# A transformer decoder layer: softmax sums inverted once a token tile and spread by way of DRAM, cross-attention in halves and quarters of the array, spline rows by indirect DMA

## The chip, the cores and the metric

The kernel runs on one NeuronCore of one Trainium2 chip. The metric is the device time of one execution in microseconds (us); less is better. The engines are PE (TensorE, matrix products), DVE (VectorE), ACT (ScalarE), POOL (GpSimd) and SP (SyncE, which here only issues DMAs). PE writes to PSUM; POOL doesn't read PSUM in this kernel.

## The reference, cut to what matters

All data is float32: four sequences of 1024 tokens with 256 features. Three sublayers follow each other, each on a normalized copy of `x` and each added to `x`:

```python
# 1. self-attention: 16 query heads, 4 key/value heads, head size 64
scores = einsum('bhqd,bhkd->bhqk', xq, xk)
probs  = softmax(scores)
out    = einsum('bhqk,bhkd->bqhd', probs, xv).reshape(B, S, 1024) @ o_w.T + o_b
# 2. cross-attention: 16 heads of size 16, 64 context tokens, masked
attn = softmax(where(mask, -inf, (q @ k.T) * 0.25))
out  = (attn @ v).reshape(b, sq, 256) @ Wout + bout
# 3. routed spline layer: each token picks one of 64 tiles
tile_idx = cluster_idx * 8 + local_idx            # two stages of argmax over calibrated scores
hh  = relu(einsum('ni,nig->ng', comp, spline_w1[tile_idx]) + spline_b1[tile_idx])
mag = einsum('ng,ngo->no', hh, spline_w2[tile_idx]) + spline_b2[tile_idx]
y   = xf + mag * directions[tile_idx] * output_scale
y   = (y - mean(y)) / sqrt(var(y) + eps) * gamma + beta
```

## The kernel before, in words

**Order of the work.** Nothing is emitted directly. Every piece of work is given to `Flow.add` (line 93) as a task with an engine, an estimated cost, a key (its place in the run), the tiles that it reads and writes, and the buffers that it holds. `Flow.order` (line 120) then plays all tasks through with those costs and emits, on each engine, whatever can start first; a `lag` is the delay that it assumes until another engine sees the result. So a changed cost or dependence reorders every engine's instructions. On the chip each engine works through its own list in order.

**Self-attention.** A sequence `b` has 8 token tiles `qt` of 128 tokens. A tile's 16 heads lie in 8 pairs of 64 partitions (`QC`), and two pairs make a `duo` (line 551): 4 duos for a tile, 32 for a sequence, 128 in all. For each pair there is one score task (line 577): four matmuls, two for each half of the array, each 64 rows by 512 columns, into two PSUM tiles `s` of 128x1024. There are two such tiles, so the next score task needs both back. DVE takes the negated row maximum `nmax` (line 591), and ACT the exponential with its row sum (line 597), which goes into `sums` and the probabilities into `prob`. In three of four duos DVE turns 32x32 blocks (line 606) and SP carries them with 16 DMAs into `probT` (line 633); in the fourth (`by_array`) PE transposes (`ptp`, line 616) and ACT copies (line 620). Then `av` (line 656) multiplies by the values, with the two heads of a pair in the two column halves of the array.

**Sums.** For each duo, DVE inverts its four sums (`rsum`, line 676). PE spreads them over partitions: four matmuls of a repeated column with the identity (`rb`, line 682). DVE copies that out of PSUM (line 691) and multiplies `av` by it into `heads` (line 695). After four duos `project` (line 702) multiplies by `wo` (`po`, line 709), adds the bias on DVE (712) and `x` on POOL (715).

**Cross-attention** (line 780) runs for two token tiles at a time. `context` builds a block-diagonal `kblk` with 8 heads per 128 partitions (`XC`), so the scores `xs` (line 819) are two matmuls of 128 rows and 512 columns for each tile. DVE adds the mask (822) and takes the maximum (834), POOL subtracts it (837), ACT takes the exponential (841), PE transposes (`pxt`, 854) and ACT copies to `xpT` (857). `xav` (line 870) then takes `xpT` as weights and `vblk` as moving operand: eight matmuls with 34 columns, 2 x 16 values and, per head, the sum. DVE inverts and divides (873, 874), PE transposes the result (`pxo`, 888), ACT copies (891) and `pxp` (900) projects.

**Spline layer** (`feed_forward`, line 991). Four token tiles at a time, at the end two. After the products with `cw1` (`pch`), `cw2` (`pcomp`) and the signatures (`pr`, line 1045) a chain of small DVE operations calibrates and picks a tile; `hot` (1075) is its one-hot row. PE transposes it (`pht`, 1089), ACT copies (1092), and a matmul with the table picks each token's row (`pg`, 1097), which ACT copies to `par` (1100).

**Normalizing** (`layernorm`, line 390): statistics on DVE (401, 402), the inverse root on POOL (406, 407), and `(x - mean) * rs` on DVE (412).

The lines of the softmax sums that the change replaces:

```python
add("DVE", 0.17, at, inverse, [ss.part(4 * e + k) for k in range(4)], [rs])
add("PE", 0.6, at + 1, spread, [rs], [pr], holds=[rb])
add("DVE", 0.42, at + 1, evict_rb, [pr], [rb])
add("DVE", 0.42, at + 1, evict, [av, rb], [heads[b, qt].part(e)])
```

Of the kernel before, what the change touches and what calls it, by code (L numbers as in the profile page):

```python
# [10 lines left out]
F32 = mybir.dt.float32  # L11
# [6 lines left out]
P = 128  # L18
# [174 lines left out]
def decoder(  # L193
# [28 lines left out]
    ps_o = ctx.enter_context(tc.tile_pool(name="ps_o", bufs=1, space=PSUM))  # L222

# [4 lines left out]
            heads=1, rb=1, rsum=2, res=1, ln=2, xxT=1, xqT=1, kblk=1, vblk=1, xkt=1, xvt=1, xsc=1,  # L228
            xmx=2, xpT=1, xrs=2, xo=1, xoT=1, xf=1, fxT=1, hT=1, sc=1, comp=2, cal=1, fm=4, hot=1, hotT=1,
            par=1, hh=1, mag=2,  # L230
        ),
        {"p1", "ln", "res", "rb", "rsum", "nmax"},
# [48 lines left out]
    tab, tab_ = load("tab", [NTILES, GT], table, "SP", -30, 8)  # L281
# [18 lines left out]
    for i in range(NCL):  # L300
        nc.gpsimd.memset(falling[:, i : i + 1], float(NCL - i))

    own = const.tile([P, XC], F32, name="own")
    nc.gpsimd.memset(own, 1.0)
    nc.gpsimd.affine_select(
        out=own, in_=own, compare_op=ALU.is_ge, fill=0.0, base=0, pattern=[[-XD, XC]], channel_multiplier=1
    )
    nc.gpsimd.affine_select(
        out=own, in_=own, compare_op=ALU.is_ge, fill=0.0, base=XD - 1, pattern=[[XD, XC]], channel_multiplier=-1
    )  # L310
# [5 lines left out]
    add("DVE", 0.2, 2, lambda: nc.vector.tensor_scalar(keep, kmask8, -1.0, 1.0, ALU.mult, ALU.add), [kmask_], [keep_])  # L316
# [40 lines left out]
    quants = buf("xo", work, 2, DC, NTILES, name="quants")  # L357
# [32 lines left out]
    def layernorm(key, name, src, dst, w, reads, writes):  # L390
# [13 lines left out]
        def rsqrt():  # L404
            _, mv, rs = st.t
            nc.gpsimd.tensor_scalar(rs, mv[:, :, 1], EPS, None, ALU.add)
            nc.gpsimd.tensor_tensor(rs, rs, minus_half.to_broadcast([P, w]), ALU.pow)

        def apply():
            _, mv, rs = st.t  # L410
            for t in range(w):
                nc.vector.tensor_scalar(dst(t), src(t), mv[:, t, 0:1], rs[:, t : t + 1], ALU.subtract, ALU.mult)
# [3 lines left out]
        add("DVE", 0.41 * w, key, apply, [st, *reads], writes)  # L416
# [134 lines left out]
    def duo(b, d):  # L551
# [3 lines left out]
        if e == 0:  # L555
            sums[b, qt] = buf("sums", small, H, name=f"sums_{b}_{qt}")
            heads[b, qt] = buf("heads", work, QC, P, name=f"heads_{b}_{qt}")
        ss = sums[b, qt]
        prob = Buf("prob", lambda: work.tile([P, 4 * S], F32, tag="prob", name=f"prob_{b}_{d}"))
# [8 lines left out]
        for i in range(2):  # L568
# [17 lines left out]
            for z in range(2):  # L586
                k = 2 * c + z
# [58 lines left out]
        for part in range(2):  # L646
            def values(part=part):
# [20 lines left out]
                holds=[heads[b, qt]],  # L668
            )

        rs = buf("rsum", small, 4, name=f"rsum_{b}_{d}")
        pr = psum1(f"rb_{b}_{d}")
        rb = buf("rb", work, 2 * P, name=f"rb_{b}_{d}")

        def inverse():
            nc.vector.reciprocal(rs.t, ss.t[:, 4 * e : 4 * e + 4])

        def spread():
            for i in range(2):
                for z, r in enumerate(halves):  # L680
                    k = 2 * i + z
                    mm(  # L682
                        pr.t[r, i * P : (i + 1) * P],
                        lhsT=rs.t[:, k : k + 1].to_broadcast([P, HD]),
                        rhs=ident,
                        start=True,
                        stop=True,
                    )

        def evict_rb():  # L690
            nc.vector.tensor_copy(rb.t, pr.t[:, : 2 * P])

        def evict():
            to = heads[b, qt].t[:, 2 * e : 2 * e + 2, :].rearrange("p c q -> p (c q)")
            nc.vector.tensor_tensor(to, av.t, rb.t, ALU.mult)  # L695

        add("DVE", 0.17, at, inverse, [ss.part(4 * e + k) for k in range(4)], [rs])
        add("PE", 0.6, at + 1, spread, [rs], [pr], holds=[rb])
        add("DVE", 0.42, at + 1, evict_rb, [pr], [rb])
        add("DVE", 0.42, at + 1, evict, [av, rb], [heads[b, qt].part(e)])  # L700

    def project(b, qt):
        at = float(b * NT * QC + qt * QC + QC + 1)
        hT, xb = heads[b, qt], x_part(b, qt)
        po, t = psum1(f"po_{b}_{qt}"), buf("res", work, D, name=f"res_{b}_{qt}")
        for part in range(2):
            def out_rows(part=part):
                for c in range(4 * part, 4 * part + 4):
                    mm(po.t[:, :D], lhsT=hT.t[:, c, :], rhs=wo[:, c, :], start=(c == 0), stop=(c == QC - 1))  # L709

            add("PE", 1.75, at, out_rows, [hT.part(e) for e in range(4)] + [wo_] + [po] * part, [po], holds=[t])
# [9 lines left out]
    def context(b, at):  # L721


        kblk = kblks[b] = buf("kblk", big, DC, XC, SK, name=f"kblk_{b}")
        vblk = vblks[b] = buf("vblk", big, XH // 2, 2, XD + 1, name=f"vblk_{b}")
# [18 lines left out]
        def block_k(c):  # L744
            nc.vector.tensor_tensor(
                kblk.t[:, c],
                kt.t[:, c, :].unsqueeze(1).to_broadcast([P, XC, SK]),
                own.unsqueeze(2).to_broadcast([P, XC, SK]),
                ALU.mult,
            )  # L750
# [13 lines left out]
        def block_v():  # L764
            vt4 = vt.t.rearrange("p (g t d) -> p g t d", t=2, d=XD)
            for half in range(2):
                r = slice(half * SK, (half + 1) * SK)
                nc.vector.tensor_scalar(vblk.t[r, :, half, :XD], vt4[r, :, half, :], keep[r, b : b + 1], None, ALU.mult)
                nc.vector.tensor_copy(vblk.t[r, :, half, XD], keep[r, b : b + 1].to_broadcast([SK, XH // 2]))
# [10 lines left out]
    def cross_attention(b, t0, at):  # L780
# [31 lines left out]
        for k in range(TX):  # L812
            now = at + 2 + 3 * k
            sc = buf("xsc", work, XH, SK, name=f"xsc_{name}_{k}")
            for c in range(DC):
                ps = psum1(f"xs_{name}_{k}_{c}")

                def scores(c=c, ps=ps, k=k):
                    mm(ps.t, lhsT=qT.t[:, c, k * P : (k + 1) * P], rhs=kblk.t[:, c], start=True, stop=True)  # L819

                def masked(c=c, ps=ps, sc=sc):
                    nc.vector.tensor_tensor(  # L822
                        sc.t[:, XC * c : XC * (c + 1), :],
                        ps.t.rearrange("p (h k) -> p h k", k=SK),
                        mneg[:, b, :].unsqueeze(1).to_broadcast([P, XC, SK]),
                        ALU.add,
                    )

                add("PE", 0.9, now, scores, [qT, kblk], [ps], holds=[sc])
                add("DVE", 0.68, now, masked, [ps, mneg_], [sc])  # L830
# [14 lines left out]
            add("ACT", 1.07, now, exponential, [sc], [sc])  # L845
            pT = buf("xpT", work, XH // 2, P, name=f"xpT_{name}_{k}")
            for g in range(2):
# [12 lines left out]
                add("ACT", 0.6, now + 2, evict, [pt], [pT])  # L860
            av = psum1(f"xav_{name}_{k}")
            rs = buf("xrs", small, XH, name=f"xrs_{name}_{k}")
            o = buf("xo", work, D, name=f"xo_{name}_{k}")

            def rows_of(av=av):
                return av.t[:, : XH * (XD + 1)].rearrange("p (h d) -> p h d", h=XH)

            def values(av=av, pT=pT, rows_of=rows_of):
                for g in range(XH // 2):
                    mm(rows_of(av)[:, 2 * g : 2 * g + 2, :], lhsT=pT.t[:, g, :], rhs=vblk.t[:, g], start=True, stop=True)  # L870

            def divide(av=av, rs=rs, o=o, rows_of=rows_of):
                nc.vector.reciprocal(rs.t, rows_of(av)[:, :, XD])
# [402 lines left out]
```

## Time and profile before

| | |
|---|---|
| median of 3 runs | 1993.22 us (1990.15 to 1993.29) |
| profiled execution | 1997.92 us, of which the span is 1996.2 us |
| mean granted TensorE clock | 0.965 |
| busy | PE 93%, DVE 77%, ACT 48%, POOL 13% |
| DMA | 220.92 MB, of which `probT` 1536 transfers of 128 KB |

In a row of costly groups one reads: the line of the kernel, the engine, the operation, the tile written and those read (with the numbers of buffers left out), the shapes, how often, then the busy time of the group and the mean of one in ns, then the idle time of the engine ahead of it and what ended most of that. A float32 matmul stands in the records as two instructions, a transpose by identity as one. A row of the chain in order of time has its start, how long it lasted, and what ran.

### The profile page before, as it was taken

To read this page: it belongs to the slowest core of one execution; us is meant where nothing else is said; L and a number is where in the kernel's file an instruction comes from. 1 tells how busy PE (TensorE), PEld (TensorE's weight loads), DVE (VectorE), ACT (ScalarE), POOL (GpSimd) and SP (SyncE) were. 2 spreads that over 40 slices of the span, in tenths; PEclk is the share of its full clock that TensorE was granted. 3 is DMA by queue.
4 is the path that set the end of the run, shared out by engine and by line. 5 is a ranking of instruction groups with operands and counts; after the bars stand their busy time and mean duration, and the time that the engine had idled before them with its cause. 6 is when DMAs were issued, how large, how long until landed. Compare 5 with 4: busy or idle time off the path is not lost.

```text
span 1996.2 us, 30371 instructions
## 1 busy us (share of the span) xinstructions
PE 1864.4 (93%) x11204; PEld 1114.0 (56%) x11204; DVE 1538.9 (77%) x2447; ACT 964.2 (48%) x1730; POOL 267.2 (13%) x422
## 2 busy tenths in 40 slices
PE   7899999999999999989999999989999999997973
PEld 4455555655566555556556555655556655564542
DVE  4767787897788878787778878887778877778853
ACT  2545455555445555545445545454545554553431
POOL 1000101030010301121000311103001030010322
PEclk9899999999999999989999999998999999998975
DMA  3555554454455455545454456535455435545510
GB/s 132 127 127 137 127 132 109 105 121 108 104 127 117 94 122 123 123 110 127 96 116 107 95 128 137 122 75 127 96 122 127 101 91 127 113 100 127 119 24 5
DMA packets 87859, 220.92 MB, mean 111 GB/s; under 512 B 26336, under 2 KB 36896, under 8 KB 87712
## 3 DMA queue, kind: packets, MB, share of 16 engines
q1 hardware_dynamic: 85440, 212.42, 47.3%
q0 software_dynamic: 1168, 4.19, 0.6%
q8 instruction: 89, 1.46, 0.3%
q10 hardware_dynamic: 1104, 2.37, 0.3%
q14 instruction: 58, 0.48, 0.1%
HBM read 13.37 MB, written 4.19 MB: 9 GB/s over the span
## 4 chain that ended last, share of the span: by engine, by line
PE 81%; DVE 12%; ACT 3%; DMA 1%; issue 1%; SPq 1%; POOL 1%; POOLq 0%; ACTq 0%; DVEq 0%
PE s L577 25%; PE av L656 22%; DVE nmax L591 6%; PE pq L530 5%; PE po L709 5%; PE ptp L616 5%; PE rb L682 2%; PE xav L870 2%; PE xs L819 2%; PE pxq L797 2%; ACT prob L597 2%; PE pv L502 2%; DVE prob L606 1%; PE pk L479 1%; PE pg L1097 1%; PE pxp L900 1%
## 5 line engine op out<-in xcount | busy, mean ns | idle before, releaser
L597 ACT ACTIVATE prob<-s,nmax 128x1024 f32<-128x1024 f32 x512 | 569.2, 1115 | 581.0 <-DVE nmax L591 571.3
L591 DVE TENSOR_REDUCE nmax<-s 128x1 f32<-128x1024 f32 x512 | 602.1, 1217 | 211.4 <-PE s L577 210.6
L577 PE MATMUL s<-kT,qT 64*128 64x512 f32 x2048 | 545.4, 621 | 9.3 <-ACT prob L597 9.0
L656 PE MATMUL av<-probT,vn 128*64 128x256 f32 x4096 | 479.6, 385 | 2.7 <-DMA probT<-prob 2.5
L606 DVE STREAM_TRANSPOSE prob<-prob 128x1024 f32<-128x1024 f32 x384 | 460.3, 1225 | 20.5 <-ACT prob L597 15.3
L656 PEld LDWEIGHTS av<-probT,vn 128*64 128x64 f32 x4096 | 284.0, 137 | 204.1 <-issue 70.5
L577 PEld LDWEIGHTS s<-kT,qT 64*128 64x128 f32 x2048 | 196.2, 187 | 216.6 <-issue 170.2
L620 ACT COPY probT<-ptp 128x512 f32<-128x512 f32 x256 | 138.9, 594 | 127.7 <-PE ptp L616 127.7
L616 PE MATMUL ptp<-ident,prob 128*128 128x128 f32 x1024 | 147.6, 281 | 20.5 <-ACT probT L620 5.0
L616 PEld LDWEIGHTS ptp<-ident,prob 128*128 128x128 f32 x1024 | 109.9, 141 | 76.4 <-issue 31.2
L530 PE MATMUL pq<-ln_T,wq 128*128 128x256 f32 x512 | 132.2, 407 | 4.2 <-DMA wq<-in_w_qT 3.7
L837 POOL TENSOR_TENSOR xsc<-xsc,xmx 128x1024 f32<-128x1024 f32 x32 | 61.0, 1908 | 497.0 <-DVE xmx L834 252.6
L709 PE MATMUL po<-wo,heads 128*128 128x256 f32 x512 | 121.1, 386 | 1.9 <-DVE xsc L822 1.8
L530 PEld LDWEIGHTS pq<-ln_T,wq 128*128 128x128 f32 x512 | 99.2, 202 | 32.8 <-issue 15.0
L709 PEld LDWEIGHTS po<-wo,heads 128*128 128x128 f32 x512 | 94.2, 190 | 34.5 <-issue 15.9
L715 POOL TENSOR_TENSOR x<-x,res 128x256 f32<-128x256 f32 x32 | 23.3, 728 | 620.9 <-DVE res L712 516.6
L597 ACT ACTIVATION_READ_ACCUMULATOR prob<-s,nmax 128x1 f32 x512 | 100.8, 197 | 0.0
L541 ACT ACTIVATE qT<-pq,bqs,qscale 128x256 f32<-128x256 f32 x128 | 65.3, 563 | 49.6 <-PE pq L530 49.2
L695 DVE TENSOR_TENSOR heads<-av,rb 128x256 f32<-128x256 f32 x128 | 53.0, 414 | 46.7 <-PE av L656 45.6
L682 PEld LDWEIGHTS rb<-ident,rsum 128*64 128x64 f32 x1024 | 54.6, 136 | 59.0 <-issue 45.4
L682 PE MATMUL rb<-ident,rsum 128*64 128x128 f32 x1024 | 83.3, 284 | 4.2 <-DVE xres L903 4.2
L819 PE MATMUL xs<-kblk,xq 128*128 128x512 f32 x128 | 67.9, 653 | 1.7 <-ACT xq L806 1.7
(162 smaller groups left out, 1526.9 us busy)
## 6 DMA issues: line engine op xcount, KB each, us to landing
probT<-prob SPq DMA_DIRECT2D x1536, 128.0 KB, 2.3
ln_n<-in_x SPq DMA_DIRECT2D x16, 256.0 KB, 3.1
x<-in_x SPq DMA_DIRECT2D x8, 512.0 KB, 4.2
out<-ln_n POOLq DMA_DIRECT2D x7, 512.0 KB, 3.5
wo<-in_w_oT SPq DMA_DIRECT2D x1, 1024.0 KB, 13.3
wq<-in_w_qT ACTq DMA_DIRECT2D x1, 1024.0 KB, 9.6
rowv<-in_rows ACTq DMA_DIRECT2D x1, 774.0 KB, 11.7
xwkv<-in_xw_kv SPq DMA_DIRECT2D x1, 512.0 KB, 13.1
```

What stands on the lines that cost most here:

```text
L530: mm(pq.t[:, 2 * P * k : 2 * P * (k + 1)], lhsT=wq[:, dc, (c + k) * P : (c + k + 1) * P], rhs=xTs[b].t[:, dc, 2 * P * w : 2 * P * (w + 1)] ...
L541: nc.scalar.activation(qTs[b, w, c + k].t, pq.t[:, 2 * P * k : 2 * P * (k + 1)], AF.Identity, bias=bqs[:, c + k : c + k + 1], scale=qscale,)
L577: mm(ps[z].t[:, 512 * g : 512 * (g + 1)], lhsT=q.t[r, (qt % 2) * P : (qt % 2 + 1) * P], rhs=kT.t[r, 512 * g : 512 * (g + 1)], start=True, ...
L591: nc.vector.tensor_reduce(nmax.t, ps[z].t, AX.X, ALU.max, negate=True)
L597: nc.scalar.activation(weights(prob.t, z, i), src, AF.Exp, bias=nmax.t, accum_out=ss.t[:, k : k + 1])
L606: nc.vector.transpose(t, t)
L616: flip(pt.t[:, j * P : (j + 1) * P], weights(prob.t, z, i)[:, kc * P : (kc + 1) * P], ident)
L620: nc.scalar.copy(to[:, z, 4 * g : 4 * g + 4, i, :], pt.t.rearrange("p (c q) -> p c q", q=P))
L656: mm(av.t[r, :], lhsT=vns[b, kc // 2].t[:, kc % 2, j * HD : (j + 1) * HD], rhs=rhs, start=(kc == 0), stop=(kc == NT - 1),)
L682: mm(pr.t[r, i * P : (i + 1) * P], lhsT=rs.t[:, k : k + 1].to_broadcast([P, HD]), rhs=ident, start=True, stop=True,)
L709: mm(po.t[:, :D], lhsT=hT.t[:, c, :], rhs=wo[:, c, :], start=(c == 0), stop=(c == QC - 1))
L819: mm(ps.t, lhsT=qT.t[:, c, k * P : (k + 1) * P], rhs=kblk.t[:, c], start=True, stop=True)
```

## The change

- **Sums.** `rb` is made once for a token tile instead of for each duo. DVE inverts all 16 sums, PE flips the 128x16 tile, ACT copies it to `rsT`, SP writes it to DRAM (`rsD`), and two more DMAs on SP read it back, each repeated over 64 partitions. `av` is copied by ACT without a factor to a buffer of its duo (five of them); POOL multiplies that by `rb`. Within a tile the sums are put in the order of the array half (`z * QC + c`).
- **Cross-attention.** `kblk` holds four heads for each half of the partitions, so that `xs` is four matmuls of 64 rows and 256 columns, the two halves into two PSUM tiles. The sums of the exponentials are taken by two halvings on POOL, a short reduction and a reciprocal on DVE, and a product on POOL, ahead of the transposes. In `xav` the values become the weights: eight matmuls of 32 columns of the array each, at column 0, 32, 64 or 96, with 128 moving columns. The result is transposed already, so `pxo` goes. `keep` is set up with five operations instead of one.
- **Spline rows.** The index of the tile is computed, and POOL's indirect DMA fetches each token's row from the table in DRAM. The one-hot transpose, its copy, the products with the table and their copies go, and so does the load of the table.
- **Normalizing.** The last step moves to ACT as `rs * x + (-mean * rs)`; POOL computes the added term with two more operations.

```diff
-            nc.vector.tensor_tensor(to, av.t, rb.t, ALU.mult)
-        add("DVE", 0.17, at, inverse, [ss.part(4 * e + k) for k in range(4)], [rs])
-        add("PE", 0.6, at + 1, spread, [rs], [pr], holds=[rb])
-        add("DVE", 0.42, at + 1, evict_rb, [pr], [rb])
-        add("DVE", 0.42, at + 1, evict, [av, rb], [heads[b, qt].part(e)])
+            nc.scalar.copy(hd.t.rearrange("p c q -> p (c q)"), av.t)
+        add("ACT", 0.45, at + 1, evict, [av], [hd])
...
+        def flip_inverse():
+            flip(pr.t[:H, :P], rs.t, ident)
+        def spread(z, r):
+            nc.sync.dma_start(out=rb.t[r], in_=rD.t[z : z + 1].to_broadcast([HD, QC, P]))
+        def divide(e):
+            nc.gpsimd.tensor_tensor(hT[e].t, hT[e].t, rb.t[:, 2 * e : 2 * e + 2, :], ALU.mult)
+        add("DVE", 0.17, at - 4, inverse, [sums[b, qt].part(k) for k in range(H)], [rs])
+        add("PE", 0.2, at - 4, flip_inverse, [rs], [pr], holds=[rT])
+        add("ACT", 0.3, at - 4, lambda: nc.scalar.copy(rT.t, pr.t[:H, :P]), [pr], [rT], holds=[rD, rb])
+        add(
+            "SP", 0.5, at - 4,
+            lambda: nc.sync.dma_start(out=rD.t.rearrange("z c q -> (z c) q"), in_=rT.t), [rT], [rD], lag=2.5,
+        )
+        for z, r in enumerate(halves):
+            add("SP", 0.5, at - 4, lambda z=z, r=r: spread(z, r), [rD], [rb.part(z)], lag=2.5)
+        for e in range(QC // 2):
+            add("POOL", 0.6, at - 1, lambda e=e: divide(e), [rb.part(0), rb.part(1), hT[e]], [hT[e]])
...
-                    mm(ps.t, lhsT=qT.t[:, c, k * P : (k + 1) * P], rhs=kblk.t[:, c], start=True, stop=True)
+                for c in range(DC):
+                    for z, r in enumerate(halves):
+                        mm(
+                            ps[z].t[:, 256 * c : 256 * (c + 1)],
+                            lhsT=qT.t[r, c, k * P : (k + 1) * P],
+                            rhs=kblk.t[r, c],
...
+            add("POOL", 1.6, now + 1, add_up, [sc], [half], holds=[rs])
+            add("DVE", 0.6, now + 1, inverse, [half], [rs])
+            add("POOL", 1.9, now + 1, divide, [sc, rs], [sc])
...
-                    mm(rows_of(av)[:, 2 * g : 2 * g + 2, :], lhsT=pT.t[:, g, :], rhs=vblk.t[:, g], start=True, stop=True)
+                        mm(
+                            av.t[32 * j : 32 * (j + 1), P * c : P * (c + 1)],
+                            lhsT=vblk.t[:, 4 * c + j].rearrange("p t d -> p (t d)"),
+                            rhs=pT.t[:, 4 * c + j, :],
+                            tile_position=(0, 32 * j),
...
-            add("PE", 0.3, now + 4, flip_o, [o], [pt], holds=[oT])
-            add("ACT", 0.38, now + 4, evict_o, [pt], [oT])
+                "ACT", 0.4, now + 3,
+                lambda av=av, oT=oT: nc.scalar.copy(oT.t.rearrange("p c q -> p (c q)"), av.t[:, :D]), [av], [oT],
...
-        add("DVE", 0.41 * w, key, apply, [st, *reads], writes)
+        add("ACT", 0.45 * w, key, apply, [st, *reads], writes)
...
-            add("PE", 0.6, at + 11, gather, [hotT, tab_], [pg], holds=[par])
-            add("ACT", 0.45, at + 11, evict, [pg], [par.part(t)])
+                nc.gpsimd.indirect_dma_start(
+                    out=par.t[:, t, :],
+                    out_offset=None,
+                    in_=table,
+                    in_offset=bass.IndirectOffsetOnAxis(ap=hot.t[3][:, t : t + 1], axis=0),
+                )
+            add("POOL", 1.2, at + 11, gather, [hot], [par.part(t)], lag=3.0)
```

## The prediction

> **What bounds the kernel now.** I read the page's shares first, then the chain that ended last, then that chain in order of time, and last the timeline around one score task.
>
> ```profile
> span 1996.2 us, 30371 instructions
> PE 1864.4 (93%) x11204; PEld 1114.0 (56%) x11204; DVE 1538.9 (77%) x2447; ACT 964.2 (48%) x1730; POOL 267.2 (13%) x422
> PE 81%; DVE 12%; ACT 3%; DMA 1%; issue 1%; SPq 1%; POOL 1%; POOLq 0%; ACTq 0%; DVEq 0%
> L682 PE MATMUL rb<-ident,rsum 128*64 128x128 f32 x1024 | 83.3, 284 | 4.2 <-DVE xres L903 4.2
> L819 PE MATMUL xs<-kblk,xq 128*128 128x512 f32 x128 | 67.9, 653 | 1.7 <-ACT xq L806 1.7
> ```
>
> PE is the bound: 93% busy and 81% of the chain. But its busy time counts pipeline ends twice. What a task really holds PE for is read from the chain in order of time, here from 780 us on (start, us, what):
>
> ```profile
> 780.03 1.90 PE xav L870 x16
> ...
> 783.81 1.92 PE s L577 x8
> ...
> 787.61 1.91 PE xs L819 x4
> 789.52 0.22 PE pxo L888 x2
> ...
> 795.31 0.59 PE rb L682 x8
> ```
>
> Priced so, every PE task of the program comes to 1783 us, so PE has 213 us with nothing to do: before the first score task (38.6 us), after the last (from 1895.7 us), and in between. What makes the holes in between is the ring score, maximum, exponential, next score (two PSUM buffers `s`):
>
> ```profile
> 730.11 1.99 PE L577 MATMUL s<-kT,qT 64*128 64x512 f32 x8
> 732.12 2.35 DVE L591 TENSOR_REDUCE nmax<-s 128x1 f32<-128x1024 f32 x2 [1.48 <-PE s L577]
> 733.44 1.11 ACT L597 ACTIVATE prob<-s,nmax 128x1024 f32<-128x1024 f32 x1 [4.70 <-DVE nmax L591]
> 734.55 1.10 ACT L597 ACTIVATE prob<-s,nmax 128x1024 f32<-128x1024 f32 x1
> ```
>
> PE leaves the score at 732.02 and its buffers are free at 735.7: 3.7 us, which PE must fill with other work. I took the PE timeline apart at the 256 score tasks and set the other work ("filler") of each of the 255 gaps beside the gap's length less 1.92. With 2.5 to 3.3 us of filler (33 gaps) a gap lasted 0.8 us beyond it; at 3.3 to 4.2 us (31 gaps) 0.5; at 4.2 to 5.6 (131 gaps) 0.4; above that nothing. In the 14 gaps above 7 us it lasted 2.9 longer, 40 us in all: PE stands there in order behind the routing of the feed-forward.
>
> ```profile
> PE pht L1089 <- DVE hot L1075: 30.1, 5, 12.8
> ```
>
> All excess comes to 138 us. So between scores: 255 x 1.92 + 1230 filler + 138 = 1857 us, which is 1895.7 - 38.6.
>
> **The change, part by part.** PE work. `rb` goes: 128 tasks of 0.59 or 0.44 (where its neighbour has its array shape), -72. In its place 32 flips of a 128x16 tile, at most 0.25 each by the 0.147 of one 128x128 flip (0.59 for four), +8. `xs` had 32 x 1.91; now each token tile issues two pairs of 64-row matmuls with 256 columns. The score task is two such pairs with 512 columns in 1.92, so 0.96 to 1.05: -29. `pxo` goes (0.22 to 0.44, 32 times): -10. `pht` (9 x 0.5) and `pg` (32 x 0.6) go: -24. `xav` had 32 x 1.90 for 16 weight loads of 128 columns; now 16 loads of 32 columns and 128 moving columns, in four column strips. No row shows quarters; the nearest is `rb`, strips of 64 with 128 columns, 8 in 0.44: at that rate 16 take 0.9. Four strips at once would be 0.5, none at once 1.9. I take 0.9, -32. Sum -159.
>
> Here a rule speaks against the change. The trace: two `pq` tasks in a row take 3.65, one alone 1.92, so a change of shape costs 0.19. The Trainium skill (TensorEngine Tiling (Array Packing), Tiling Modes) says the same thing more strictly, that a switch of tiling mode drains TensorE, which would charge the quarters with an extra stop. By the row it is 2 x 0.19 x 32 = 12 us, but `xav` between scores paid it before as well and `rb` (128 switches) goes, so I add nothing.
>
> The gaps. I read the new filler off the order in which the built program issues on PE. It falls to 1089 us in 255 gaps, none above 7 us. By class: 11 hold nothing (1 before) and cost 3.7 each, 41; 14 hold about 2.2 and cost the 1.5 that is missing to 3.7, 22; 37 at 2.5 to 3.3 cost 0.9, 33; 46 at 3.3 to 4.2 cost 0.5, 23; 107 at 4.2 to 5.6 cost 0.33, 36; 40 above cost 2. That is 157 us. Read in the same way, the order of before gives 112 where its trace shows 98 outside the 14 long gaps, so I take 14 off. So the 40 us behind `pht` go, and shorter cover takes 45 back. Between scores: 490 + 1089 + 143 = 1722.
>
> New waits on PE. (a) The new order puts `pxp` at most 1.7 us behind `xav` in 24 of 32 cases (2 before), with only an ACT copy between (371 ns for this shape, row `xoT`), which can stand behind two exponentials (2.2). 24 x 0.7 = 17, between 0 and 40. Likewise `xs` stands directly behind `pxq` in 9 of 16 cases (3 before), 6 x 1.2 = 7. (b) The inverse's way: flip 0.25, ACT copy 0.3, SP issue, landing, two more issues, landing, two POOL products. From
>
> ```profile
> 869.52 10.66 SPq L633 DMA_DIRECT2D probT<-prob  x15
> ln_n<-in_x SPq DMA_DIRECT2D x16, 256.0 KB, 3.1
> out<-ln_n POOLq DMA_DIRECT2D x2, 256.0 KB, 2.6
> L715 POOL TENSOR_TENSOR x<-x,res 128x256 f32<-128x256 f32 x32 | 23.3, 728 | 620.9 <-DVE res L712 516.6 <-DVE rsum L676 83.5 <-DVE lm_m L984 20.7
> ```
>
> an issue is 0.7, a write 2.6, a spread 3.1, a product 0.73: 0.25 + 0.3 + 0.7 + 2.6 + 1.4 + 3.1 + 1.46 + 0.3 of hand-overs = 10.1 us. What PE has between that flip and `po` in its own order is about 11 us in 13 token tiles, 15 in four and 18 to 22 in 14 (the last lies in the tail): hidden, with 1 us to spare in the 13; 13 x 0.6 = 8. Behind SP's wait for the write stand the two spreads and the next duo's 16 carries, which `av` needs; its transposes end some 13 us after the tile's last exponential, and SP is free by 10: nothing, or 0.2 us per us of delay that reaches them. SP issues 96 DMAs more, 67 us on a queue that waited 742 us for `prob`; landing adds 16 MB to 221 MB.
>
> Other engines. DVE: -53 (`rb` copies), -53 (`heads`), -14 (reciprocals), -55 (normalizing), -21 (`xo`, `xrs`), +27 (32 x (619 + 240) ns), +10 (four 128x256 masks of 414 against two of 681): -159, 1380. ACT: +47 (128 copies of 371), +72 (128 normalizings at 563, the row with bias and scale), +10, -18: +111, 1075, and table loads stay 18, five of them now ahead of an exponential (5 x 1.28 = 6 us, half felt: 3). POOL: 128 x 0.73 = 93, halves 59, divisions 32 x 1.9 = 61, two small operations per normalization 42, 32 gathers at 0.85 (the row of its own DMA issue) 27: +282, 549. None reaches 75% of the new span.
>
> A second rule bears on POOL. Its rows lie at 728, 730, 734 and 727 ns for one shape while DVE is 77% busy, so no contention shows. The Trainium skill (GPSIMD Engine Reference, Key points) says GpSimd shares its SBUF interfaces with VectorE, with contention from DVE instructions with two SBUF inputs. By the row +0. By the rule: DVE's groups with two SBUF inputs (the `cal` steps, `par`, `kblk` and the like) add up to some 85 us, 4% of the span, so even if POOL stood still beside them, 12 of its added 282 us, on an engine off the path. Either way nothing is added.
>
> Cross-attention's way from `xs` to `pxt` grows by 1.85 + 0.86 + 1.9 - 0.4; PE's work in between grows from about 12.5 to 15.9 us in the new order: nothing.
>
> Head: the last `pv` tasks move behind the first score, -3.6. Tail (100.5 us): the weight of `pht` and `pg` ahead of the last cross-attention goes (-3); each of its two tiles gains 4.6 for sums and division and loses about 2 in `xs`, 1 in `xav`, 1 in `pxo` and its copies: +2; the gather (two issues, landing 2.6) replaces 4.2 us: 0; normalizing +1.5 twice: +3. Sum +2.
>
> Sum: 35.0 + 1722 + 17 + 7 + 8 + 3 + 102.5 = 1894.5. The gap classes hold part of (a) already, since a wait inside a gap shorter than the ring costs nothing; a third of the gaps are that short, so I take 11 off: span 1884. Around the span lie 1.7 us (1997.9 - 1996.2), and the profiled run stood 4.7 above the median: 1884 + 1.7 - 4.7 = 1881, 5.6% less.
>
> **The rivals.** First, nearly all comes through: DVE, lighter by a tenth, answers the scores sooner, and the excess stays 98 instead of 143 + 35 - 11: 1881 - 69 = 1812 at best. Against: the 3.7 us are the operations themselves. Second, quarters don't overlap and ACT holds `pxp` up: 32 + 23 = 55, 1936. Third, slower: the DRAM way decides. If it takes T, PE stands still T - 11 in 13 tiles, T - 15 in four and T - 18 in 14, with scores behind it. The gain of 112 is used up at T = 18.3 (95 + 13 + 4 = 112); at 20 it is 117 + 20 + 28 = 165, so 1881 + 165 = 2046. For it: the spreads share rings with 2 MB of carries, and SP serves in order. Against: the last duo of a tile has no carries, and nothing in the trace lands later than 4.2 us in the steady part.
>
> **How the numbers follow.** The forecast 0.74; the first rival 0.10; the second 0.11; the third 0.05. The forecast's own ends are quarters at 0.5 and no new waits (1881 - 13 - 24 = 1844) and (a) at 40 instead of 17 with (b) and the table loads at twice their size (1881 + 23 + 11 = 1915). The range 1838 to 1930 leaves out the first rival's better part, the third and the second's worse half. Within 0.2% (4 us, what a measurement can tell) hardly any case falls: 0.01; faster 0.94.
>
> **What would show it.** `xs` near 1.0 and `xav` near 0.9 per tile in the chain; no wait of PE on the feed-forward; DVE near 73%, ACT 57%, POOL 29%; `pxp` waiting for the copy by tens of us in all. A wait of `po` on POOL in tens of us, or carries late behind SP's waits, would make it wrong.

## The result, and the profile after

The changed kernel takes 1979.4 us (median of six runs, 1971.4 to 1982.4) beside 1994.6 for the kernel before on the same chip (1990.2 to 1998.5): a ratio of 0.9913, 95% interval 0.9894 to 0.9931. It is faster by 15 us. The forecast said 112 us faster than the median it was given, and the time lies outside its range of 1838 to 1930.

The first lines of the page of after are span, busy time and the chain that ended last:

```profile
span 1976.4 us, 28894 instructions
PE 1737.7 (88%) x10180; PEld 1025.7 (52%) x10180; DVE 1400.9 (71%) x2036; ACT 1062.5 (54%) x1977; POOL 554.1 (28%) x872
PE 64%; DVE 16%; ACT 6%; POOL 5%; DMA 3%; SPq 3%; issue 3%; POOLq 0%; DVEq 0%; ACTq 0%
```

PE lost 127 us of busy time, but its share of the chain fell from 81% to 64%: other engines now end last for a third of the span. The groups by line show the new PE work, and the chain in order of time shows what a task holds PE for (start, us, what):

```profile
L837 PE MATMUL xs<-kblk,xq 64*128 64x256 f32 x256 | 41.7, 434 | 12.9 <-ACT xq L823 12.9
L913 PE MATMUL xav<-xpT,vblk 128*32 128x128 f32 x512 | 21.4, 285 | 0.1
L704 PE MATMUL rsT<-ident,rsum 128*16 128x128 f32 x32 | 8.8, 277 | 0.0
L728 PE MATMUL po<-wo,heads 128*128 128x256 f32 x512 | 119.2, 383 | 1.6 <-POOL heads L710 1.6
```

```profile
212.17 0.57 PE xav L913 x16
...
214.67 0.91 PE xs L837 x8
```

The quarters overlap almost fully (0.57 for 16 matmuls, where the estimate for four at once was 0.5), `xs` takes 0.91, and `po` hardly waits for the inverse that comes by DRAM (1.6 us in all). The work is near the forecast, with `xav` and `xs` somewhat cheaper. The waits of PE are not (us in all, times, longest):

```profile
PE ln_pt L441 <- ACT ln_n L427: 42.4, 14, 7.8
PE s L592 <- ACT prob L612: 34.6, 22, 3.3
PE ptp L631 <- ACT prob L612: 30.4, 17, 2.6
PE av L671 <- DMA probT<-prob: 26.0, 9, 4.9
PE pxt L898 <- POOL xsc L885: 20.8, 2, 11.3
```

The same cut of the PE timeline at the 256 score tasks, now with 0.57 and 0.91 for the new tasks (a gap's excess is its length less 1.92 and less its filler, so a score that runs slowly counts as excess too):

| | before | forecast | after |
|---|---|---|---|
| first score starts at | 38.6 | 35.0 | 36.8 |
| scores, 255 x 1.92 | 490 | 490 | 490 |
| filler | 1230 | 1089 | 1088 |
| excess and new waits | 138 | 167 | 251 |
| behind the last score's start | 100.5 | 102.5 | 110.4 |
| span | 1996.2 | 1884 | 1976.4 |

By these prices the filler is right within 1 us. That has luck in it, since `xav` and `xs` came out some 13 us cheaper than the forecast priced them, and something else made it up. Priced by the median step from one matmul to the next, the filler is 1233 us before and 1066 after, and the excess 134 and 274. So the split between the two is good to some 25 us, and their sum is firm. The excess takes back 113 of the 141 us of filler that left. By class of filler:

| filler of the gap | gaps | forecast excess | after |
|---|---|---|---|
| none | 11 | 41 | 31 |
| up to 2.5 | 17 (14 forecast) | 22 | 13 |
| 2.5 to 3.3 | 34 (37) | 33 | 28 |
| 3.3 to 4.2 | 51 (46) | 23 | **124** |
| 4.2 to 5.6 | 102 (107) | 36 | 39 |
| above | 40 | 2 | 16 |

So one class holds the miss, and four kinds of gap hold 102 of its 124 us. Here is PE around one sequence's end, with two of them:

```profile
613.29 2.16 PE L592 MATMUL s<-kT,qT 64*128 64x512 f32 x8
618.71 4.91 PE L592 MATMUL s<-kT,qT 64*128 64x512 f32 x8 [3.25 <-ACT prob L612]
623.55 4.18 PE L671 MATMUL av<-probT,vn 128*64 128x256 f32 x32
627.66 1.99 PE L592 MATMUL s<-kT,qT 64*128 64x512 f32 x8
633.81 0.33 PE L441 MATMUL ln_pt<-ident,ln_n 128*128 128x128 f32 x1 [4.17 <-ACT ln_n L427]
634.30 0.55 PE L441 MATMUL ln_pt<-ident,ln_n 128*128 128x128 f32 x3 [0.17 <-ACT ln_n L427]
635.53 3.78 PE L814 MATMUL pxq<-ln_T,xwq 128*128 128x256 f32 x8 [0.68 <-ACT ln_T L444]
639.87 2.08 PE L837 MATMUL xs<-kblk,xq 64*128 64x256 f32 x8 [0.56 <-ACT xq L823]
```

1. **Behind empty gaps, 34 us in nine gaps.** Eleven gaps hold nothing, and PE idles in them for 2.43 to 3.26 us. The score behind an empty gap takes 3.11 us even at the full clock, because its second buffer comes 1.1 us after the first, with the second exponential. In ten of the eleven the clock has fallen as well, and the score takes 4.12 to 4.91 us (three scores took over 4 us before). A score with both buffers free at the full clock takes 1.99. Here is the one at full clock, then its stretch and that of the score at 618.71; the third figure from the right is the granted clock:

```profile
277.61 3.11 PE L592 MATMUL s<-kT,qT 64*128 64x512 f32 x8 [2.43 <-ACT prob L612]
277.61:280.72 3.11, 3.10 (x10) 1.04 (x12) 3.04 (x7) 1.52 (x3) 1.38 (x4) 1.00 0.32 91
618.71:623.62 4.91, 4.91 (x10) 2.01 (x12) 4.28 (x10) 1.08 (x2) 1.10 (x1) 0.50 0.79 192
```

   So some 10 of the 34 us (nine times 1.1) are the wait for the second buffer, and some 24 are the clock. Its mean over the run fell from 0.965 to 0.939. The Trainium skill (TensorE: Matmul & The Clock Gate, Part 1: The HAM clock gate) puts the fall behind about one idle window of 3.4 us. By that figure none of the eleven gaps would pay; ten did, from 2.43 us on.
2. **`ln_pt`, `pxq`, `xs` with nothing between them, 26.5 us in three gaps.** PE waits 4.17, 0.68 and 0.56 us, and runs `pxq` and `xs` at half clock on top (3.78 and 2.08). ACT at that moment shows why:

```profile
630.93 1.11 ACT L612 ACTIVATE prob<-s,nmax 128x1024 f32<-128x1024 f32 x1 [2.78 <-DVE nmax L606]
632.07 1.11 ACT L612 ACTIVATE prob<-s,nmax 128x1024 f32<-128x1024 f32 x1
633.17 1.08 ACT L427 ACTIVATE ln_n<-x,ln_mv,ln_rs 128x256 f32<-128x256 f32 x2
```

   POOL had the normalizing's bias ready at 629.95, and ACT was idle. But `ln_n` stands in ACT's queue behind two exponentials of a score that PE had only issued at 627.66. So `ln_pt` can't come before 1.99 + 1.2 + 2.3 + 0.6 us from there.
3. **`av` waiting for its carries, 28 us in four gaps, one a sequence** (4.38, 4.40, 4.33 and 4.90 us, and half clock behind each). The way is 16 issues on SP after the second transposes. In the first of the four, SP issues carries from 382.4 on and `av` starts at 394.4, while PE has other work only until 390.1.
4. **`ptp` waiting for an exponential, 13 us in four gaps.**

### The profile page after: what moved, and what is told of

Same layout as the page of the kernel before. It is cut to its first block, busy times and chain, and to the rows that moved or that the text cites. A ratio compares the mean times of both kernels' runs of the same rounds, so it can differ in the third digit from the quotient of the medians.

```text
span 1976.4 us, 28894 instructions
## 1 busy us (share of the span) xinstructions
PE 1737.7 (88%) x10180; PEld 1025.7 (52%) x10180; DVE 1400.9 (71%) x2036; ACT 1062.5 (54%) x1977; POOL 554.1 (28%) x872
## 4 chain that ended last, share of the span: by engine, by line
PE 64%; DVE 16%; ACT 6%; POOL 5%; DMA 3%; SPq 3%; issue 3%; POOLq 0%; DVEq 0%; ACTq 0%
PE s L592 22%; PE av L671 18%; DVE nmax L606 6%; PE pq L545 5%; PE po L728 4%; PE ptp L631 4%; DVE prob L621 3%; SPq L648 3%; ACT prob L612 3%; PE pk L494 1%; PE pv L517 1%; DMA par<-in_table,tile 1%; PE pxt L898 1%; PE xs L837 1%; PE pxq L814 1%
## 5 line engine op out<-in xcount | busy, mean ns | idle before, releaser
L592 PE MATMUL s<-kT,qT 64*128 64x512 f32 x2048 | 584.4, 639 | 35.0 <-ACT prob L612 34.6
L671 PE MATMUL av<-probT,vn 128*64 128x256 f32 x4096 | 499.4, 396 | 29.5 <-DMA probT<-prob 26.0
L671 PEld LDWEIGHTS av<-probT,vn 128*64 128x64 f32 x4096 | 298.2, 142 | 252.3 <-issue 111.7
L592 PEld LDWEIGHTS s<-kT,qT 64*128 64x128 f32 x2048 | 212.9, 192 | 266.5 <-issue 163.6
L710 POOL TENSOR_TENSOR heads<-heads,rb 128x256 f32<-128x256 f32 x128 | 90.0, 729 | 607.6 <-DMA rb<-rsD 503.7
L631 PE MATMUL ptp<-ident,prob 128*128 128x128 f32 x1024 | 141.1, 281 | 34.0 <-ACT prob L612 30.4
L427 ACT ACTIVATE ln_n<-x,ln_mv,ln_rs 128x256 f32<-128x256 f32 x64 | 36.6, 596 | 107.1 <-POOL ln_mv L422 107.1
L686 ACT COPY heads<-av 128x256 f32<-128x256 f32 x128 | 47.6, 372 | 76.3 <-PE av L671 73.9
L419 POOL TENSOR_SCALAR ln_rs<-ln_mv 128x1 f32<-128x1 f32 (+1 forms) x96 | 21.4, 222 | 213.2 <-DVE ln_mv L415 200.7
L441 PE MATMUL ln_pt<-ident,ln_n 128*128 128x128 f32 x192 | 37.2, 312 | 44.9 <-ACT ln_n L427 42.4
```

Of the source, the lines that this page charges most:

```text
L592: mm(ps[z].t[:, 512 * g : 512 * (g + 1)], lhsT=q.t[r, (qt % 2) * P : (qt % 2 + 1) * P], rhs=kT.t[r, 512 * g : 512 * (g + 1)], start=True, ...
L631: flip(pt.t[:, j * P : (j + 1) * P], weights(prob.t, z, i)[:, kc * P : (kc + 1) * P], ident)
L671: mm(av.t[r, :], lhsT=vns[b, kc // 2].t[:, kc % 2, j * HD : (j + 1) * HD], rhs=rhs, start=(kc == 0), stop=(kc == NT - 1),)
L710: nc.gpsimd.tensor_tensor(hT[e].t, hT[e].t, rb.t[:, 2 * e : 2 * e + 2, :], ALU.mult)
```

## The experiments

"Before" was run beside each kernel on its chip, and its median moved between 1994.1 and 1998.6. So differences between runs are taken from the ratios, times 1996 us; with intervals of about 0.003 on either side one run's difference from before is good to some 6 us, and that of two runs from each other to some 8.

**The parts.** A is the sums by way of DRAM, B cross-attention in halves and quarters, C the spline rows by indirect DMA, D the normalizing on ACT. A was not run alone. Undoing D:

```
-                nc.scalar.activation(dst(t), src(t), AF.Identity, bias=mv[:, t, 1:2], scale=rs[:, t : t + 1])
+                nc.vector.tensor_scalar(dst(t), src(t), mv[:, t, 0:1], rs[:, t : t + 1], ALU.subtract, ALU.mult)
```

> The changed kernel with the last step of normalizing back on DVE (and without POOL's two extra operations); all else as changed. Theory L, normalizing's longer way over POOL and ACT holds PE in order at `ln_pt`: the gaps between scores that hold `ln_pt` lose most of their excess, some 30 us, so about 1950. Theory C, PE's half clock behind gaps that hold nothing is the main loss: the order shifts, but as many empty gaps remain, 1979 within 10. Rival: DVE, 55 us busier, answers the scores later, 1990.

Undoing A (back to `rb` and a reciprocal once a duo):

> The changed kernel with the sums as before: inverted for each duo, spread by PE (`rb`), multiplied on DVE; no way through DRAM. PE's work is 64 us more. Theory W (PE's work sets the time, as the prediction had it): 1979 + 64 = 2043. Theory C: that work stands in the gaps, empty gaps go and with them 70 us, about 1975. Theory D (the way through DRAM holds SP, and carries behind it come late): carries no longer late, excess falls by more than the 64, about 1955.

The parts by themselves:

> The kernel of before with the cross-attention part alone (halves for `xs`, quarters for `xav`, sums taken and divided ahead of the transposes). Theory W: 71 us of PE work go, about 1927. Theory G: the way from `xs` to `xpT` is 4 us longer, and the gaps around it were partly shorter than the ring: 1985 to 2005.

> The kernel of before with one part of the change alone: the spline rows by indirect DMA. Theory W (PE's work sets the time): 24 us of work and the 40 us of waits behind `pht` go, about 1934. Theory G (what counts are the gaps: cover, and what PE waits for in order): the waits behind `pht` go, but the gather's chain moves to POOL, and normalizing waits there; about 1965.

> The kernel of before with the cross-attention and the spline rows changed; sums by PE for each duo and normalizing on DVE as before. From the runs so far, if the parts add up: this lies 28 below the one with normalizing on ACT besides (2010), so about 1981; and 30 above the one with the new sums besides (1952). Theory W: 135 us less than before, 1863.

> The kernel of before with normalizing's last step on ACT alone. Theory W: PE's work is the same, 1998. Theory L (normalizing's longer way holds PE in order): about 27 us more, as with the other parts in place, 2025. Rival: DVE, 55 us lighter, answers the scores sooner, 1985.

| parts | median us | ratio, 95% interval | filler less than before | excess more than before |
|---|---|---|---|---|
| B | 2003.6 | 1.0056 (1.0036 to 1.0075) | 66 | 63 |
| C | 1995.5 | 1.0002 (0.9988 to 1.0016) | 22 | 17 |
| B, C | 1992.1 | 0.9987 (0.9969 to 1.0005) | 87 | 77 |
| D | 2020.4 | 1.0139 (1.0119 to 1.0158) | -2 | 15 |
| B, C, D | 2009.9 | 1.0051 (1.0035 to 1.0067) | 79 | 80 |
| A, B, C | 1951.9 | 0.9760 (0.9721 to 0.9798) | 151 | 97 |
| A, B, C, D | 1979.4 | 0.9913 (0.9894 to 0.9931) | 141 | 113 |

Theory W, that PE's work sets the time, missed in every one of these runs with less or more PE work. A undone came to 2010 us, where no theory had it (W 2043, C 1975, D 1955). B alone lies in theory G's range, C alone is 30 us above G, and B with C is 11 above the sum of the parts.

What a part is worth depends on what it is added to. A pays: 45 us on top of B and C (0.9987 - 0.9760), 28 on top of B, C and D. With A, 64 us of filler leave and excess rises by 20. C gains nothing alone and 14 us on top of B (1.0056 - 0.9987); B alone is 11 slower. B and C together take 87 us of work off PE between the scores, and 77 come back as excess. D costs 28 us alone, 13 on top of B and C, and 31 on top of A, B and C, although it takes 45 to 58 us off DVE. What the two columns leave lies ahead of the first score and in the tail: there B alone loses 8 us, C 4 and D 6. What happens to C's gain is seen in the waits. Before, `ln_pt` waited for `ln_n` as follows, beside the 30.1 us of `pht`, and `ptp` for ACT's copies:

```profile
PE ln_pt L426 <- DVE ln_n L412: 16.5, 6, 6.7
PE ptp L616 <- ACT probT L620: 5.0, 16, 0.8
```

C alone:

```profile
PE ln_pt L425 <- DVE ln_n L411: 42.9, 13, 6.8
PE av L655 <- DMA probT<-prob: 12.7, 4, 10.4
```

`pht` is gone, and its 30 us with it; `ln_pt` waits 26 us more and `av` 10, in one piece. And D alone, where 0.6 us pieces of normalizing now stand among the copies and exponentials in ACT's queue:

```profile
PE ptp L618 <- ACT probT L622: 24.5, 19, 3.2
PE pht L1091 <- DVE hot L1077: 16.6, 2, 12.8
PE ln_pt L428 <- ACT ln_n L414: 11.7, 3, 7.5
```

`ptp` waited 5.0 us for ACT's copies before and waits 24.5 now, while `pht` and `ln_pt` wait 18 us less; so the rise of `ptp` alone does not make up what D costs. Alone, D came out near theory L (2020 us for 2025), but PE is not held at `ln_pt` for it, as L has it.

On top of A, B and C, taking D back came out at L's number too (1951.9 us for about 1950), and not by its mechanism either. With the normalizing on DVE, `ln_pt` waits longer than the 42.4 us that it waited for ACT, and at a sequence's end it waits 6.92 instead of 4.17 (three times in either kernel):

```profile
PE ln_pt L439 <- DVE ln_n L425: 51.7, 11, 7.6
636.35 1.23 PE L439 MATMUL ln_pt<-ident,ln_n 128*128 128x128 f32 x4 [6.92 <-DVE ln_n L425]
```

The gaps that hold `ln_pt` keep their excess (67 us for 68). So both hits were luck. Other waits shrank in the new order (`s` from 34.6 to 28.3 us, `av` from 26.0 to 20.2), and what the 31 us are made of stays open.

**The clock behind empty gaps.** Where two score tasks follow each other with nothing between, four idle matmuls into an unused half of a PSUM bank go ahead of the second:

```
+                if t.lead and last is not None and last.lead:
+                    self.fill()
...
+            for _ in range(4):
+                mm(latest[-1][:, 2 * P :], lhsT=ident, rhs=wq[:, 0, : 2 * P], start=True, stop=True)
```

> The changed kernel, same order, with four idle matmuls (identity by 256 columns, about 1.7 us) issued on PE in ten of the eleven gaps between two score tasks that hold no other work; their result is not read. Theory C, the half clock: the score behind such a gap falls from about 4.9 us to 2 to 3.1 and the `av` behind it from 4.2 to 6.0 to 3.7; ten times 3.5 is 35 us, so about 1945. Theory O (the order is planned with costs that don't fit the chip, waits for carries and copies are the main loss): nothing gained, 1979 within 5, or up to 10 us lost since the idle work can end after the buffers are free.

1960.9 us, 0.9806 (0.9775 to 0.9837): 21 us less than the changed kernel, with 17 us of idle work added. The clock is 0.951, and none of the ten slow scores is left: a score behind a filled gap takes 3.11 us at a granted clock of 1.00, with the wait for its second buffer still in it. (One score takes over 4 us, but that one stands behind `ptp`.) The excess is 35 lower, of which 17 is the idle work that now counts as filler. So it is shown that the clock behind empty gaps costs about 20 us, near the 24 read from the trace.

**The planner's costs.** Seven costs set to what the trace shows (a carry 0.75 instead of 0.6, a spread's landing 3.9 instead of 2.5, and so on):

> The changed kernel with the planner's costs and delays set to what its trace shows (a carry 0.75 instead of 0.6 us, a spread's landing 3.9 instead of 2.5, POOL products 0.75, normalizing on POOL 1.6 and on ACT 0.6 per tile, the halvings 1.9, the gather's landing 4.1); same work in another order. Theory O: the waits of `av` for carries (about 41 us in PE and weight loads), of `ln_pt` and of `ptp` shrink by half, about 1945. Theory C: what counts is how many empty gaps the new order has; with as many as now 1979 within 12.

1978.9 us, 0.9897 (0.9868 to 0.9925): no difference. The waits for carries left the head of the list, and longer ones of `s` and `pxq` came: excess 252 as against 251.

**Is either engine the bound?** The order of issue is kept (the planner's entries and costs stay), and work is left out of one engine. Half of `po`:

```
-                for c in range(4 * part, 4 * part + 4):
+                for c in range(4 * part, 4 * part + 2):
```

Less on DVE:

```
-        ... (1.0, lambda: picked(0)), (1.0, lambda: picked(1)), (0.4, value)):
+        ... (1.0, None), (1.0, None), (0.4, None)):
```

> The changed kernel with its order of issue kept, but each token tile's output projection multiplies only chunks 0, 1, 4 and 5 of the heads by wo (4 of the 8 chunks, 8 of 16 matmuls), so 61 us of PE work (32 x 1.9) are left out and nothing else. Theory P (PE's work and the ring of scores set the time, with the cover rule of the prediction): the gaps that hold po get shorter, some fall below 3.7 us and give part back; by the rule 37 us come through, 1979 - 37 = 1942. Theory V (DVE's queue, served in order, paces the score tasks, and work taken off PE alone comes back as waiting): at most 15 us, 1964 to 1979.

> The changed kernel with its order of issue kept, but both gate calibrations of the feed-forward leave out their table lookup (five of the eleven DVE operations of each: two products with 224 columns, two sums, and the two small ones behind them), so about 72 us of DVE work are left out (32 x (2 x 0.39 + 2 x 0.54 + 2 x 0.19)) and nothing on PE. Theory V: the waits of av for carries (four of 4.4 us, 29 us with the slow clock behind them) and the ln_pt to pxq to xs stretches (33 us) go, since DVE has no hole from 374 to 398 us and from 607 to 622; 1979 - 45 to - 65 = 1914 to 1934. Theory P: those waits are a matter of order and turn up elsewhere; at most 20 us, 1959 to 1979.

> Both of the last two at once: half of po's matmuls and the calibrations' table lookups left out, order of issue kept. Theory V: more than the sum of the two, since PE's lighter work can only come through once DVE is lighter: 1979 - 90 to - 110 = 1869 to 1889. Theory P: the sum, 1979 - 37 - 10 = 1932, 1915 at best.

> The kernel before, order of issue kept, each output projection over 4 of the 8 head chunks only: 61 us of PE work left out. On the changed kernel the same cut gave 20 us (1979.4 to 1959.4). Theory P (the kernel before is bound by PE, and the change used that up): by the cover rule of the prediction 44 of the 61 us come through, about 1996 - 44 = 1952. Theory Q (both kernels stand in waits that the fixed order of the queues sets, and PE's work counts for a third in either): 1996 - 20 = 1976.

> The kernel before, order of issue kept, with the table lookup of both gate calibrations left out: 72 us of DVE work less. On the changed kernel the same cut gave 23 us. Theory P: DVE is off the path before, so only the 30 us behind pht can shrink; 1996 - 0 to - 12 = 1984 to 1996. Theory Q: a third as there, 1996 - 23 = 1973.

The second cut is smaller than the expectations say. They count 32 calibrations of 2.24 us; the traces have 18 (108 DVE instructions fewer, six for each). DVE's busy time fell by 37 us in the changed kernel (1400.9 to 1363.6) and by 36 in the kernel before, not by 72.

| | PE 61 us lighter | DVE 37 us lighter | both |
|---|---|---|---|
| kernel before | 1968.7, 0.9855 (0.9811 to 0.9898): -29 | 1993.3, 0.9980 (0.9965 to 0.9995): -4 | |
| changed kernel | 1959.4, 0.9792 (0.9753 to 0.9832): -24 | 1956.3, 0.9792 (0.9758 to 0.9826): -24 | 1943.7, 0.9722 (0.9686 to 0.9758): -38 |

Neither theory wins whole. The kernel before answers to DVE by next to nothing (4 of 36 us), as theory P has it, and to PE by about half of the relief (29 of 61 us, good to 9: below the 44 of P, and the 20 of Q lies at its edge). The changed kernel gives 24 of 61 us for PE and 24 of 37 for DVE, good to some 8. So it has become sensitive to DVE, which the kernel before was not. Theory V's share for DVE (45 to 65 of 72) would make 23 to 33 of 37, and P had at most 20, so this run doesn't tell them apart. Both cuts together give 38, no more than the sum, against theory V. What theory V said of the places is wrong too. With DVE lighter the long waits stand where they stood:

```profile
397.75 4.50 PE L671 MATMUL av<-probT,vn 128*64 128x256 f32 x24 [4.27 <-DMA probT<-prob]
...
634.43 1.39 PE L441 MATMUL ln_pt<-ident,ln_n 128*128 128x128 f32 x4 [4.17 <-ACT ln_n L427]
636.50 3.78 PE L814 MATMUL pxq<-ln_T,xwq 128*128 128x256 f32 x8 [0.68 <-ACT ln_T L444]
```

`ln_pt` waits 4.17 us to the hundredth in all three runs: the changed kernel, DVE lighter and PE lighter. So the load of neither engine makes this wait. ACT's rows above show what does in this order: a place in a queue that is fixed when the kernel is built. A task stands behind another that waits for a score just issued, and so inherits the score's way through DVE and ACT.

**Where the normalizing stands, and the fastest version.**

> The changed kernel with the layer normalizing back on DVE, and four idle 256-column matmuls at the start of each gap between two score tasks that holds nothing. The first alone gave 1951.9, the second alone took 18.5 off the changed kernel. If the two causes (ACT's queue behind the normalizing, and the clock that falls behind empty gaps) are separate: 1952 - 14 (there are 9 empty gaps instead of 11) = 1938. If the idle matmuls only fill time that DVE takes anyway: 1952.

> The fastest version so far (1940.7: everything but the ACT normalizing, and idle matmuls in empty gaps), with the layer normalizing on POOL instead of DVE: 128 operations of about 0.75 us move there, DVE loses about 55 us. If relief of DVE counts for a third wherever it comes from: 1941 - 18 = 1923. If what counts is whom a normalizing stands behind in its queue (on ACT behind two exponentials, on DVE behind a maximum, on POOL behind products of 1.9 us and gathers): no gain, 1941 to 1960.

A, B, C and the idle matmuls: 1940.7 us (1935.0 to 1946.2), 0.9720 (0.9691 to 0.9750), the fastest measured, 2.8% below the kernel before and 39 us below the changed one. By themselves the two remedies gain 31 and 21, together 39: on top of the first, the idle matmuls bring 8 us, where 14 were expected, and 8 is not clear of the noise. With the normalizing on POOL it is 1959.0, 0.9797 (0.9754 to 0.9840), 15 slower (good to some 11), though DVE loses 59 us (1400 busy instead of 1459): moving it off DVE costs on ACT and on POOL alike. Each move also makes the planner issue in another order, so how much of these 31 and 15 us is the queue and how much the order can't be told from these runs.

**How much an order is worth.** The same edit on the fastest version and on the kernel before, and a third of it:

```
-                        "SP", 0.6, at, carry, ...
+                        "SP", 0.75, at, carry, ...
```

> The fastest version so far (1940.7) with the planner told that SP takes 0.75 us for the issue of a carry instead of 0.6 (the traces show about 0.65 to 0.7), so that it places av later behind the transposes. If the four waits of av for its carries (21.6 us and the slow clock behind them) can be filled by an order with later av: 1941 - 20 = 1921. If another wait takes their place, as in the run with all costs corrected: 1941 within 5.

> The kernel before with the planner told 0.75 us for the issue of a carry instead of 0.6, which changes its order of issue and no work. On the version that took this in the last run (less work, thinner cover) the same edit cost 55 us. Theory T (thin cover: an order is only worth much where PE has little work to cover waits with): the kernel before, with more PE work between its scores, stays within 10 us of 1996.5. Theory U (any order of this planner is a draw, whatever the cover): it moves by over 20 us, to below 1976 or above 2017.

> The fastest version (1940.7 with 0.6 for a carry, 1995.7 with 0.75) with 0.65 for a carry. If the cost acts by degrees (av later, more waits elsewhere): a third of the way, 1955 to 1963. If each cost draws another order: anywhere between 1935 and 2000, and not near 1959.

With 0.75 the fastest version goes to 1995.7 us, 0.9986 (0.9973 to 0.9998), and the kernel before to 2050.9, 1.0247 (1.0219 to 1.0276): 53 and 49 us slower with no work added. With 0.65 it stays at 1945.2, 0.9722 (0.9695 to 0.9750). So theory T falls, since the kernel before suffers as much, and it moves as theory U said. "By degrees" falls as well: at a third of the way the time hardly moves. In the kernel before the filler is the same (1231), and the excess grew from 138 to 191, most of it in gaps of 3.3 to 5.6 us. The wait that grew most is that of `ptp` for ACT's copies, 5.0 us before:

```profile
PE ptp L616 <- ACT probT L620: 21.5, 35, 1.1
```

That the loss is alike in both kernels speaks somewhat against a mere draw, though two runs can't rule it out. Why the planner's order gets worse between 0.65 and 0.75 stays open, and so does why the changed kernel with D bore the 0.75 among its seven costs without loss.

## Why the prediction was wrong

- **PE work: right, to 1 us by luck.** Forecast -159 in all, of which 141 between the scores; the filler came out at 1088 for 1089. `xav` was taken at 0.9 and took 0.57, `xs` 0.96 to 1.05 and took 0.91. The second rival, that quarters do not overlap and ACT holds `pxp` up, is out on both counts: `pxp` waits 4.9 us.
- **The way by DRAM: right.** `po` waits 1.6 us for POOL. The spread landed in 3.9 us (3.1 taken), the write in 1.4 (2.6 taken). From the flip at 368.1 to POOL's first product at 377.0 it is 8.8 us, and two products make it 10.3, with 10.1 forecast. The slower rival, which turned on it, is out, and A gained 28 to 45 us.
- **Other engines: right.** DVE 1401 for 1380, ACT 1062 for 1075, POOL 554 for 549.
- **The gaps: wrong, and this is the step that failed.** "46 at 3.3 to 4.2 cost 0.5, 23": there were 51, and they cost 124. The price was the average of gaps of that length in the kernel before. But the new order put other tasks into them: four `av` directly behind their carries, three chains of `ln_pt`, `pxq` and `xs` with nothing between, nine scores and `av` behind an empty gap. The length of a gap's filler says whether the ring of the scores is covered. It says nothing on whether the filler itself is ready.
- **"So the 40 us behind `pht` go": misread, and what went came back.** Of the 30.1 us that the prediction shows for `pht`, 14.6 lie in the tail and 9.7 in one other gap; in the 14 long gaps it is 2.9 us, twice. So their 40 us were not one wait that could be taken out. The long gaps did go, but the prediction named no successor. C alone shows it: `ln_pt` and `av` wait 36 us more.
- **Empty gaps at 3.7 each: right for the gap, short for what follows.** They cost 31 for 41. The 1.1 us that each score then waits for its second buffer are counted in the next gap; with them it is 43. The clock behind them cost some 24 more. The prediction had score rows of a fallen clock in its own trace (three over 4 us) and put nothing on the clock behind eleven empty gaps; filling ten of them gave 21 us net.
- **The normalizing on ACT: undersized.** 3 us between the scores and 3 in the tail were forecast, for table loads and a longer operation. It cost 13 to 31, by what it was added to. The prediction counted ACT's busy time (57%) and not what stands ahead of `ln_n` in its queue, nor what `ln_n` stands ahead of. That ACT's queue made the cost is not shown: back on DVE, `ln_pt` waits longer.
- **(a): about right in sum, wrong in its parts.** 17 and 7 us were taken for `pxp` and `xs`; they waited 4.9 and 12.9. The prediction's own sign, `pxp` waiting for the copy by tens of us, did not come.
- **The tail: 110.4 for 102.5.** `pxt` waits 20.8 us for POOL's products there, with nothing beside it. The kernel before had 6.3 us of waits for ACT at that place, nearly all of it in the tail.

The sum: +84 between the scores, +1.8 in the head, +7.9 in the tail, makes up the 92 us by which the profiled span exceeds 1884 (the rest is rounding).

## What to carry to other kernels

When work leaves an engine that covers waits, price each gap by what is in it and by when that is ready, not by an average over gaps of its length, and for every wait that is removed name the task that is late next. Where queues are served in order, read for each moved instruction which unready one it will stand behind: an engine at 54% can hold the busiest one up, and adding idle matmuls to keep the clock paid where gaps were empty. When a run hits its expected number, look whether the wait named in the expectation went; here a run hit and the wait had grown. Before a part is credited with a gain, see what a change of order alone does; here one planner cost, with no work changed, was worth 50 us.

## What the runs showed of the hardware

- The length of an idle stretch alone did not set how far the clock fell. Behind 2.43 us the granted clock of the next score was 1.00, 0.74 and 0.61 (3.11, 4.12 and 4.50 us for the score), behind 2.46 to 3.26 us it was 0.50 (4.91). In the run with idle matmuls the first such gap, left empty, idled 2.46 us too, and there the clock was 1.00 (3.11). In the kernel before, 1.87 us was enough for 0.73 (4.32).
- A score starts when its first PSUM buffer is free and waits 1.1 us within itself for the second: 3.11 us at full clock for 1.99.
- Matmuls in four column strips overlap almost fully: 16 with 128 moving columns took 0.57 us, while 8 of `rb` in two strips took 0.44 to 0.59.
- A write of 8 KB from 16 partitions to DRAM landed in 1.4 us and its broadcast over 64 partitions in 3.9; an indirect DMA held POOL for 0.95 to 1.1 us and landed in 4.1:

```profile
rb<-rsD SPq DMA_DIRECT2D x64, 256.0 KB, 3.9
rsD<-rsT SPq DMA_DIRECT2D x32, 8.0 KB, 1.4
par<-in_table,tile POOLq DMA_INDIRECT x32, 4.1
```
